# One-hot expert selection of a Flamingo block on one Trainium2 core: compares in 16 bits with token pairs innermost, the weight fold moved around the first choices, and runs of 8 tokens

## The chip, the cores and the metric

The kernel runs on one core of one Trainium2 chip. The metric is the device time of one launch in microseconds (us); the kernel before takes 4431.82 us, the median of 3 runs (4430.32 to 4437.95). One more execution was taken with the hardware profiler; all rows and stage times come from it.

## What is computed

Two Flamingo layers over x of 8 sequences, 512 tokens and 256 features. Each adds a tanh-gated cross-attention and a tanh-gated feed-forward to x. The change lies in the second feed-forward, a product-key memory of 64 x 64 = 4096 experts, cut here to what matters:

```python
q = einsum('bnd,de->bne', x, w_q)                       # 2 halves x 8 heads x 128
q = (q - mean) * rsqrt(var + eps) * gamma + beta        # statistics over all tokens
sim = einsum('pbnhd,hkpd->pbnhk', q, keys)              # 2 x 8 heads x 64 keys per token
sx, ix = top_k(sim[0], 8); sy, iy = top_k(sim[1], 8)
scores, pk = top_k(sx[..., :, None] + sy[..., None, :], 8)   # 8 of the 64 pairs of each head
indices = 64 * ix + iy, taken at pk                     # 64 experts per token
h = softmax(scores) * gelu_new(x . down_embed[indices])
out = sum over the 64 experts of h * up_embed[indices]
```

## The kernel before

**Stages.** `attention_phase` does everything up to the last feed-forward and, while it runs, computes the inner products of x with all 4096 `down` rows for seven of the eight sequences (`inner`, `expert_products`, L123), storing them to DRAM in `h_d`. `fold_phase` then does the same for the last sequence (`activations`, 16 calls, GELU straight into the tiles `gs`), and folds w_q, the batch statistics and the keys into one matrix `mk` and one row `crow` (matmuls into `y`, `sq`, `pw`, `pc`). The last stage walks over 16 blocks of 256 tokens, two tiles p of 128 tokens each, four steps u per tile.

**One step of the last stage.** `one_hot` (L1250, L1252) compares the tokens' 64 chosen first and second key numbers (`chT`) with 0..63 (`iota`) on VectorE (DVE), giving `m1` and `m2` of 128 x 1024 in fp32, and GpSimd (POOL) multiplies `m2` by the softmax weight (L1253). 32 matmuls of 64 x 64 (L1263) turn them into the weight of every expert for 16 tokens, `cf` in PSUM. `weigh` (L1272, DVE) multiplies the activations `gs` by them in place. `finish` (L1281) multiplies the previous block's `gs` by `up_sb`, in six pieces over steps 0 to 5 of a block; after step 5 `store` adds x and writes `out` (`fin`, L1296, L1299), and reads the next block's x rows (`xt`, L1293). For tiles ahead, `similar` makes the similarities (L1162, L1163, copied to `sim` by ScalarE, ACT, L1164), `top` finds 8 of 64 in 16 rows (L1175, L1176), `choose` 8 of 64 pairs in 8 rows (L1192, L1193) and `places` the key numbers (L1206 to L1239). `fetch` (L1304) loads four pieces c0 to c3 of the block after next from `h_d` into `gs` when `finish` has freed them, and `apply` (L1310) runs GELU on them on ACT.

**Order.** Only TensorE (PE) keeps the order in which the code is written; for the other engines and SP's DMA queue a scheduler fixes an order when the program is built, and each runs its own in sequence. In the built order ACT copies a tile's second `sim` half after the GELUs of c0 and c1. The DMAs of the queues take eight semaphores in turn, so each waits for the one eight places before it. Tokens are split over the two column halves of the PE array in runs of 32 (`s=32`), which fixes that `xt` and `out` move in DMAs of 32 rows, 8 each per block. The whole of `up` (two copies, 8.4 MB) is loaded from POOL's queue ahead of the fold, L1133.

Of the kernel before, what the change touches and what calls it, by code (L numbers as in the profile page):

```python
# [36 lines left out]
def kernel(  # L37
# [79 lines left out]
    def expert_products(ps, dw, xT):  # L117


        for k in range(NK):  # L120
            runs = xT[:, k, :].rearrange("p (r q s) -> p r q s", q=2, s=32)
            for q in range(2):
                nc.tensor.matmul(  # L123
                    ps[64 * q : 64 * q + 64, :], dw[:, k, :], runs[:, :, q, :],
                    start=(k == 0), stop=(k == NK - 1),
                )
# [905 lines left out]
    def fold_phase(ctx: ExitStack):  # L1032

        wp = ctx.enter_context(tc.tile_pool(name="wp", bufs=2))
        st = ctx.enter_context(tc.tile_pool(name="st", bufs=1))
        ps_h = ctx.enter_context(tc.tile_pool(name="ps_hl", bufs=2, space=PSUM))
        ps_y = ctx.enter_context(tc.tile_pool(name="ps_yf", bufs=2, space=PSUM))
        ps_s = ctx.enter_context(tc.tile_pool(name="ps_st", bufs=1, space=PSUM))

        xl = st.tile([P, NK, S], F32, name="xl")  # L1040
        nc.sync.dma_start(xl, xT_d[:, :, last * S : (last + 1) * S])
        bn_sb = st.tile([P, 32], F32, name="bn_sb")
        nc.scalar.dma_start(bn_sb, bn)
        kT = st.tile([P, 16, 64], F32, name="kT")
        nc.scalar.dma_start(kT, keysT)

        def activations(i4):

            dw = wp.tile([P, NK, 4, 64], F32, name="dwl")
            nc.sync.dma_start(dw, down[:, :, 4 * i4 : 4 * i4 + 4, :])  # L1050
            for i2 in range(2):
                ps = ps_h.tile([P, 2, 2 * P], F32, name="ps_hl")
                for ii in range(2):
                    expert_products(ps[:, ii, :], dw[:, :, 2 * i2 + ii, :], xl)
                for n in range(2):
                    i0 = 4 * i4 + 2 * i2
                    nc.scalar.activation(
                        gs[n][:, i0 : i0 + 2, :], ps[:, :, n * P : (n + 1) * P],
                        AF.Gelu_apprx_tanh,
                    )  # L1060


        sq = ps_s.tile([P, 16, 2], F32, name="sq")
        for n4 in range(4):
            wq = wp.tile([P, NK, 512], F32, name="wq")
            nc.scalar.dma_start(
                wq, pwq[:, 512 * n4 : 512 * (n4 + 1)].rearrange("(k p) n -> p k n", p=P)
            )
            z = wp.tile([P, NK, 512], F32, name="z")
# [1 line left out]
            for k in range(NK):
                y = ps_y.tile([P, 512], F32, name="y", tag="y")
                for k2 in range(NK):
                    nc.tensor.matmul(
                        y, gram[:, k2, k * P : (k + 1) * P], wq[:, k2, :],
                        start=(k2 == 0), stop=(k2 == NK - 1),
                    )
                nc.vector.tensor_tensor(z[:, k, :], y, wq[:, k, :], ALU.mult)
# [1 line left out]
            for i in range(4):  # L1080
                n = 4 * n4 + i
                for j, (src, by) in enumerate(((z, None), (wq, gram))):
                    for k in range(NK):
                        nc.tensor.matmul(
                            sq[:, n, j : j + 1], src[:, k, i * P : (i + 1) * P],
                            ones[:, 0:1] if by is None else by[:, k, D : D + 1],
                            start=(k == 0), stop=(k == NK - 1),
                        )
        mv = st.tile([P, 16, 2], F32, name="mv")
        nc.vector.tensor_scalar(mv, sq, 1.0 / (NT * P), None, ALU.mult)  # L1090

        sc = st.tile([P, 16], F32, name="bn_sc")
        sh = st.tile([P, 16], F32, name="bn_sh")
        nc.vector.tensor_tensor(sc, mv[:, :, 1], mv[:, :, 1], ALU.mult)
        nc.vector.tensor_tensor(sc, mv[:, :, 0], sc, ALU.subtract)
        nc.vector.tensor_scalar(sc, sc, 0.0, EPS_LN, ALU.max, ALU.add)
        nc.gpsimd.tensor_tensor(sc, sc, mhalf.to_broadcast([P, 16]), ALU.pow)
        nc.vector.tensor_tensor(sc, sc, bn_sb[:, 0:16], ALU.mult)
        nc.vector.tensor_tensor(sh, sc, mv[:, :, 1], ALU.mult)
        nc.vector.tensor_tensor(sh, bn_sb[:, 16:32], sh, ALU.subtract)  # L1100
        ks = st.tile([P, 16, 64], F32, name="ks")
        nc.vector.tensor_tensor(ks, kT, sc.unsqueeze(2).to_broadcast([P, 16, 64]), ALU.mult)
        kh = st.tile([P, 16, 64], F32, name="kh")
        nc.vector.tensor_tensor(kh, kT, sh.unsqueeze(2).to_broadcast([P, 16, 64]), ALU.mult)
# [2 lines left out]
        for h in range(2):
            pw = [ps_y.tile([P, 8, 64], F32, name="pw", tag="y") for _ in range(NK)]
            for q4 in range(2):
                wT = wp.tile([P, 4, D], F32, name="wT")  # L1110
                nc.scalar.dma_start(wT, pwqT[:, 8 * h + 4 * q4 : 8 * h + 4 * q4 + 4, :])
                for k in range(NK):
                    for i in range(4):
                        nc.tensor.matmul(
                            pw[k][:, 4 * q4 + i, :], wT[:, i, k * P : (k + 1) * P],
                            ks[:, 8 * h + 4 * q4 + i, :], start=True, stop=True,
                        )
            for k in range(NK):
                nc.vector.tensor_copy(
                    mk[:, k, 512 * h : 512 * h + 512].rearrange("p (n i) -> p n i", i=64), pw[k]  # L1120
                )
        for h in range(2):
            pc = ps_y.tile([P, 512], F32, name="pc", tag="y")
            nc.tensor.matmul(
                pc[0:1], ones[:, 0:1], kh[:, 8 * h : 8 * h + 8, :].rearrange("p n i -> p (n i)"),
                start=True, stop=True,
            )
            nc.vector.tensor_copy(crow[:, 512 * h : 512 * h + 512], pc[0:1])
# [22 lines left out]
    def similar(p, h):  # L1151
# [89 lines left out]
    def one_hot(p, u):

        at = cts[p].rearrange("p x (q s) -> p x q s", q=2)[:, :, :, 8 * u : 8 * u + 8]

        def spread(x):
            return at[:, x].unsqueeze(3).to_broadcast([P, 2, 8, 64])

        grid = iota.unsqueeze(1).unsqueeze(1).to_broadcast([P, 2, 8, 64])
        m1 = oh.tile([P, 2, 8, 64], F32, name="m1")
        nc.vector.tensor_tensor(m1, spread(0), grid, ALU.is_equal)  # L1250
        m2 = oh.tile([P, 2, 8, 64], F32, name="m2")
        nc.vector.tensor_tensor(m2, spread(1), grid, ALU.is_equal)  # L1252
        nc.gpsimd.tensor_tensor(m2, m2, spread(2), ALU.mult)  # L1253
# [61 lines left out]
    for p in range(2):
        for h in range(2):
            similar(p, h)
        for n0 in (0, 8):
# [81 lines left out]
```

## Time and profile before

| | us |
|---|---|
| median of the runs shown | 4431.82 |
| profiled execution, its own time | 4438.74 |
| its span, first to last instruction | 4436.9 |
| end of the attention stage (last `ps_g` matmul ended) | 3311.4 |
| first `sim` matmul of the last stage | 3458.6 |
| first `cf` matmul | 3510.6 |
| first `fin` | 3613.9 |
| last `cf` matmul / last `acc` matmul | 4400.8 / 4430.2 |
| busy: PE, DVE, ACT, POOL | 85%, 56%, 36%, 14% |

The page averages over stages with different limits: DVE is busy 56% of the whole, but 98.6% of the time from 3750 to 3900 us. Busy times by stretch, and instructions in order of time, are read below.

### The profile page before, as it was taken

The numbers are of one execution on the slowest core, as the hardware profiler recorded it, in microseconds if no ns is written. First come the engines' busy times: TensorE is split into PE (matmuls) and PEld (weight loads), VectorE is DVE, ScalarE is ACT, GpSimd is POOL, SyncE is SP. The second block draws the span as 40 slices with busy tenths as digits, with TensorE's granted clock in tenths as the row PEclk, the third lists the DMA queues.
The fourth block names the chain that finished last, engine by engine and source line by source line (L and its number), as shares of the span: only waits on it lengthen the run. The fifth ranks groups of instructions, "written<-read, shape, count | busy, mean of one in ns | idle before, by whom it ended". The sixth has DMA issues, their size and how long they took to land.

```text
span 4436.9 us, 74250 instructions
## 1 busy us (share of the span) xinstructions
PE 3779.7 (85%) x30697; PEld 1922.5 (43%) x30697; DVE 2473.8 (56%) x5662; ACT 1580.1 (36%) x2029; POOL 616.8 (14%) x613
## 2 busy tenths in 40 slices
PE   5678788889888998998898898789987589999998
PEld 2223332434334344434334434234445266666667
DVE  3455544454554454455445534553200699999995
ACT  2124343334443443453354343443431123333221
POOL 3210101020011012002001200000000122222222
PEclk7678998899999999999999999998997799999999
DMA  3201122123113313311321321103353022222221
GB/s 97 50 20 39 32 65 53 39 69 103 54 54 105 89 46 99 101 48 54 107 77 51 103 87 46 26 23 81 100 158 95 15 78 84 90 92 92 84 90 42
DMA packets 192254, 314.79 MB, mean 71 GB/s; under 512 B 20190, under 2 KB 145662, under 8 KB 184510
## 3 DMA queue, kind: packets, MB, share of 16 engines
q1 hardware_dynamic: 173468, 239.98, 18.0%
q0 software_dynamic: 15776, 65.02, 5.3%
q10 hardware_dynamic: 2672, 5.04, 0.4%
q8 instruction: 242, 3.96, 0.4%
q14 instruction: 96, 0.79, 0.1%
HBM read 220.93 MB, written 88.24 MB: 70 GB/s over the span
## 4 chain that ended last, share of the span: by engine, by line
PE 37%; DVE 17%; DMA 3%; ACT 1%; issue 1%; POOL 1%; SPq 0%; DVEq 0%; POOLq 0%; ACTq 0%
PE sc L331 10%; PE acc L1281 7%; PE ps_hd L123 6%; DVE nm L348 4%; PE av L391 3%; DVE m L1250 2%; DVE gs L1272 2%; DVE m L1252 2%; PE ps_y L707 1%; PE ps_hl L123 1%; DVE i L1176 1%; PE ps_h L690 1%; PE ps_sim L1162 1%; PE ps_q L293 1%; PE cf L1263 1%
## 5 line engine op out<-in xcount | busy, mean ns | idle before, releaser
L348 DVE TENSOR_REDUCE nm<-sc 128x2 f32<-128x1024 f32 x768 | 939.1, 1224 | 1047.0 <-PE sc L331 1043.2
L331 PE MATMUL sc<-ka,qa 32*128 32x512 f32 x3072 | 960.7, 684 | 297.4 <-DVE nm L348 284.4
L376 ACT ACTIVATE pr<-sc 128x1024 f32<-128x1024 f32 x768 | 785.9, 1024 | 1156.9 <-PE sc L331 1155.1
L331 PE MATMUL sc<-qa,ka 32*128 32x512 f32 x3072 | 917.8, 671 | 21.0 <-ACT pr L376 15.9
L331 PEld LDWEIGHTS sc<-ka,qa 32*128 32x128 f32 x3072 | 261.2, 194 | 722.7 <-DVE nm L348 535.8
L1281 PE MATMUL acc<-up_sb,gs 64*128 64x256 f32 x4096 | 489.9, 394 | 37.6 <-DVE gs L1272 37.6
L123 PE MATMUL ps_hd<-xT,dw 128*64 128x256 f32 x3584 | 439.0, 390 | 17.0 <-DMA dw<-in_down 6.5
L1281 PEld LDWEIGHTS acc<-up_sb,gs 64*128 64x128 f32 x4096 | 405.0, 195 | 93.3 <-DVE gs L1272 39.8
L391 PE MATMUL av<-pr,v 128*32 128x512 f32 x3072 | 436.6, 642 | 7.1 <-ACT pr L376 7.1
L1253 POOL TENSOR_TENSOR m<-m,chT 128x1024 f32<-128x1024 f32 x128 | 256.8, 2006 | 724.1 <-DVE m L1252 513.7
L123 PEld LDWEIGHTS ps_hd<-xT,dw 128*64 128x64 f32 x3584 | 247.1, 139 | 248.8 <-issue 117.9
L331 PEld LDWEIGHTS sc<-qa,ka 32*128 32x128 f32 x3072 | 246.8, 190 | 69.9 <-ACT pr L376 34.6
L823 ACT COPY hb<-ps_hd 128x512 f32<-128x512 f32 x224 | 130.8, 586 | 314.9 <-PE ps_hd L123 289.4
L542 ACT ACTIVATE pd<-mb,aT 128x512 f32<-128x512 f32 (+3 forms) x256 | 129.6, 553 | 211.2 <-PE cav L549 108.7
L391 PEld LDWEIGHTS av<-pr,v 128*32 128x32 f32 x3072 | 62.0, 110 | 320.2 <-issue 298.7
L534 POOL TENSOR_SCALAR_AFFINE_SELECT mb<-mb 128x256 f32<-128x256 f32 x128 | 52.2, 408 | 1010.9 <-DMA mb<-nM_d 572.8
L1263 PE MATMUL cf<-m,m 64*64 64x64 f32 x8192 | 156.1, 228 | 34.5 <-DVE gs L1272 29.0
L1263 PEld LDWEIGHTS cf<-m,m 64*64 64x64 f32 x8192 | 138.9, 141 | 101.4 <-issue 84.8
L1250 DVE TENSOR_TENSOR m<-chT,iota 128x1024 f32<-128x1024 f32 x128 | 169.8, 1326 | 2.0 <-ACT chT L1239 2.0
L569 DVE SCALAR_TENSOR_TENSOR pd<-csc,pd 128x512 f32<-128x512 f32 (+3 forms) x256 | 115.9, 486 | 94.3 <-PE csc L564 77.5
L1196 ACT ACT_TABLE_LOAD x28 | 35.9, 1283 | 366.5 <-DVE w L1195 354.3
L564 PE MATMUL csc<-qT,cT 32*128 32x256 f32 (+3 forms) x512 | 150.8, 567 | 10.8 <-DVE pd L569 7.2
(218 smaller groups left out, 4330.9 us busy)
## 6 DMA issues: line engine op xcount, KB each, us to landing
h_d<-hb SPq DMA_DIRECT2D x224, 256.0 KB
gs<-h_d SPq DMA_DIRECT2D x56, 1024.0 KB
dw<-in_down SPq DMA_DIRECT2D x112, 256.0 KB
w1e<-in_w POOLq DMA_DIRECT2D x16, 1024.0 KB, 5.4
w2e<-in_w POOLq DMA_DIRECT2D x16, 1024.0 KB, 6.3
mb<-nM_d SPq DMA_DIRECT2D x32, 512.0 KB
qk_d<-pk SPq DMA_DIRECT2D x64, 256.0 KB
ws<-in_w SPq DMA_DIRECT2D x56, 256.0 KB
```

Source lines behind the costliest of these rows:

```text
L123: nc.tensor.matmul(ps[64 * q : 64 * q + 64, :], dw[:, k, :], runs[:, :, q, :], start=(k == 0), stop=(k == NK - 1),)
L331: nc.tensor.matmul(sc[:, i, :], lhs[r : r + 32, g, c * P : (c + 1) * P], rhs[r : r + 32, g, :], start=True, stop=True,)
L348: nc.vector.tensor_reduce(self.nm[:, c, 2 * half : 2 * half + 2, g], sc, AX.X, ALU.max, negate=True)
L376: nc.scalar.activation(self.pr[jj], sc, AF.Exp)
L391: nc.tensor.matmul(self.av[32 * j : 32 * j + 32, :], self.va[:, c, h * (self.hd + 1) : h * (self.hd + 1) + 32], pr[j // 2][:, j % 2, :], s ...
L542: nc.scalar.activation(pds[c][:, i, s0:], mb[:, i, s0:], AF.Exp, bias=aT[:, c, h : h + 1])
L564: nc.tensor.matmul(sc[i][:, s0:], cT[r : r + 32, g, s0 : s0 + P], qT[r : r + 32, g, s0:], start=True, stop=True,)
L823: nc.scalar.copy(hb.rearrange("p n i t -> p i n t"), ps.rearrange("p i (n t) -> p i n t", n=2),)
L1250: nc.vector.tensor_tensor(m1, spread(0), grid, ALU.is_equal)
L1253: nc.gpsimd.tensor_tensor(m2, m2, spread(2), ALU.mult)
L1263: nc.tensor.matmul(cf[64 * q : 64 * q + 64, h, s, :], m2[rows, q, s, :], m1[rows, q, s, :], start=True, stop=True,)
L1281: nc.tensor.matmul(accs[n][q], gs[n % 2][rows, i, :], up_sb[rows, i, :], start=(i == 0), stop=(i == 63),)
```

## The change

- **Fold.** `activations` for experts 0..5 stay in the fold; the other ten calls stand behind the similarities, `top` and `choose` of the first two tiles, five before each `places`. The fold's inputs are loaded at its start into the room of `up_sb`, and `up` is loaded afterwards in 16 DMAs of 0.5 MB on SP's queue, whose order is now that of the code in this phase. The column sums `pc` come right behind the statistics.
- **`crow`** becomes three bf16 rows that add up to the fp32 row, multiplied by bf16 ones.
- **`one_hot`** compares bf16 against bf16 into `o1`, `o2`, with a pair of tokens innermost; ACT copies `o1` to fp32 `m1`, POOL multiplies `o2` by the weight into fp32 `m2`. The buffers: `o1` 1, the others 2, where `m1` and `m2` had 3. The 64 x 64 matmuls read `m1` and `m2` with a step of two elements.
- **Small work** goes from DVE to ACT (`kf`, `iv`) and to POOL (`w`, the softmax product).
- **Runs of 8** (`s=8`) in place of 32: `xt` and `out` move in 32 DMAs each of 8 rows per block.

```diff
-            runs = xT[:, k, :].rearrange("p (r q s) -> p r q s", q=2, s=32)
+            runs = xT[:, k, :].rearrange("p (r q s) -> p r q s", q=2, s=8)
...
-        nc.tensor.matmul(ps, ones[0:1, :], crow[:, cols], start=False, stop=True)
+        nc.tensor.matmul(ps, ones3, crow[:, cols], start=False, stop=True)
...
-        nc.vector.tensor_tensor(w, sc, sc[:, :, 0:1].to_broadcast([P, 8, 8]), ALU.subtract)
+        nc.gpsimd.tensor_tensor(w, sc, sc[:, :, 0:1].to_broadcast([P, 8, 8]), ALU.subtract)
...
-        nc.vector.tensor_copy(kf, ku)
+        nc.scalar.copy(kf, ku)
-        nc.vector.tensor_copy(iv, i8)
+        nc.scalar.copy(iv, i8)
...
-            activations(2 * n4)
+            activations(n4)
...
-            activations(2 * n4 + 1)
...
-        for i4 in range(8, 12):
-            activations(i4)
...
-        for i4 in range(12, 16):
-            activations(i4)
-    for q in range(2):
-        nc.gpsimd.dma_start(up_sb[64 * q : 64 * q + 64], up)
...
+                pc[0:3], ones[:, 0:3], kh[:, 8 * h : 8 * h + 8, :].rearrange("p n i -> p (n i)"),
+                start=True, stop=True,
...
+        activations(4)
+        activations(5)
...
+        for p in range(2):
+            for h in range(2):
+                similar(p, h)
+            for n0 in (0, 8):
+                top(p, n0)
+            choose(p)
+        for p in range(2):
+            for i4 in range(5 * p + 6, 5 * p + 11):
+                activations(i4)
+            places(p)
+            for i in range(32 * p, 32 * p + 32, 8):
+                for q in range(2):
+                    nc.sync.dma_start(
+                        up_sb[64 * q : 64 * q + 64, i : i + 8, :], up[:, i : i + 8, :]
+                    )
+        for h in range(2):
+            similar(2, h)
...
-        nc.vector.tensor_tensor(m1, spread(0), grid, ALU.is_equal)
-        nc.vector.tensor_tensor(m2, spread(1), grid, ALU.is_equal)
-        nc.gpsimd.tensor_tensor(m2, m2, spread(2), ALU.mult)
+        def tokens(x):
+            x = x[:, 16 * u : 16 * u + 16].rearrange("p (v t) -> p v t", t=2)
+            return x.unsqueeze(2).to_broadcast([P, 8, 64, 2])
+        grid = iota.unsqueeze(1).to_broadcast([P, 8, 64, 2])
+        o1 = oh.tile([P, 8, 64, 2], BF16, name="o1", bufs=1)
+        nc.vector.tensor_tensor(o1, tokens(ci[:, 0]), grid, ALU.is_equal)
+        m1 = oh.tile([P, 8, 64, 2], F32, name="m1")
+        nc.scalar.copy(m1, o1)
+        o2 = oh.tile([P, 8, 64, 2], BF16, name="o2")
+        nc.vector.tensor_tensor(o2, tokens(ci[:, 1]), grid, ALU.is_equal)
+        m2 = oh.tile([P, 8, 64, 2], F32, name="m2")
+        nc.gpsimd.tensor_tensor(m2, o2, tokens(cw), ALU.mult)
...
-            for r in range(4):
-                row = t0 + 64 * r + 32 * q
+            for r in range(16):
+                row = t0 + 16 * r + 8 * q
```

More of the change, by code (lines that the diff above doesn't have):

```diff
@@ L1015 @@
     mk = p2.tile([P, NK, 1024], F32, name="mk")
-    crow = p2.tile([1, 1024], F32, name="crow")
+    crow = p2.tile([3, 1024], BF16, name="crow")
+    ones3 = p2.tile([3, P], BF16, name="ones3")
+    nc.vector.memset(ones3, 1.0)
     iota8 = p2.tile([P, 8], BF16, name="iota8")
-    iota = p2.tile([P, 64], F32, name="iota")
+    iota = p2.tile([P, 64, 2], BF16, name="iota")
     nc.gpsimd.iota(
@@ L1023 @@
     nc.gpsimd.iota(
-        iota, pattern=[[1, 64]], base=0, channel_multiplier=0,
+        iota, pattern=[[1, 64], [0, 2]], base=0, channel_multiplier=0,
         allow_small_or_imprecise_dtypes=True,
@@ L1030 @@
     tiles = [2 * n + i for n in blocks for i in range(2)]
[L1032 to L1069, printed above, removed]
-            activations(2 * n4)
[L1071 to L1078, printed above, removed]
-            activations(2 * n4 + 1)
[L1080 to L1104, printed above, removed]
-        for i4 in range(8, 12):
-            activations(i4)
[L1107 to L1128, printed above, removed]
-        for i4 in range(12, 16):
-            activations(i4)
@@ L1132 @@
-    for q in range(2):
-        nc.gpsimd.dma_start(up_sb[64 * q : 64 * q + 64], up)
-    ctx.enter_context(tc.manual_schedule(engines=ORDERED))
-    with ExitStack() as phase:
-        fold_phase(phase)
     tk = ctx.enter_context(tc.tile_pool(name="tk", bufs=2))
-    oh = ctx.enter_context(tc.tile_pool(name="oh", bufs=3))
-    ps_c = ctx.enter_context(tc.tile_pool(name="ps_c", bufs=2, space=PSUM))
-    ps_o = ctx.enter_context(tc.tile_pool(name="ps_o", bufs=1, space=PSUM))
+    oh = ctx.enter_context(tc.tile_pool(name="oh", bufs=2))
@@ L1228, in places @@
         nc.vector.reciprocal(sm, sm)
-        nc.vector.tensor_tensor(
+        nc.gpsimd.tensor_tensor(
             mlw[:, 2, 0, :].rearrange("p (h k) -> p h k", k=8), w,
@@ L1236, in places @@
             nc.tensor.transpose(tr[:, i, :], mlw[:, i].rearrange("p d k -> p (d k)"), ident)
-        ct = cts[p] = tk.tile([P, 3, 64], F32, name="chT", bufs=3)
-        nc.scalar.copy(ct[0:64], tr[0:64, 0:3, 0:64])
-        nc.scalar.copy(ct[64:128], tr[64:128, 0:3, 64:128])
-    def one_hot(p, u):
[L1243 to L1253, printed above, removed]
+        ci = tk.tile([P, 2, 64], BF16, name="ciT", bufs=3)
@@ new lines, in places, with fold_phase, room, activations @@
+        cw = tk.tile([P, 64], F32, name="cwT", bufs=3)
+        for h in range(2):
+            rows = slice(64 * h, 64 * h + 64)
+            nc.scalar.copy(ci[rows], tr[rows, 0:2, rows])
+            nc.scalar.copy(cw[rows], tr[rows, 2, rows])
+        cts[p] = (ci, cw)
+    def fold_phase(ctx: ExitStack):
+        wp = ctx.enter_context(tc.tile_pool(name="wp", bufs=2))
+        st = ctx.enter_context(tc.tile_pool(name="st", bufs=1))
+        ps_h = ctx.enter_context(tc.tile_pool(name="ps_hl", bufs=2, space=PSUM))
+        ps_y = ctx.enter_context(tc.tile_pool(name="ps_yf", bufs=2, space=PSUM))
+        ps_s = ctx.enter_context(tc.tile_pool(name="ps_st", bufs=1, space=PSUM))
+        def room(i, shape):
+            axes = dict(zip("ab", shape))
+            return up_sb[:, 4 * i : 4 * i + 4, :].rearrange(
+                "p x y -> p (x y)"
+            ).rearrange("p (a b) -> p a b", **axes)
+        xl = room(15, (NK, S))
+        nc.sync.dma_start(xl, xT_d[:, :, last * S : (last + 1) * S])
+        bn_sb = st.tile([P, 32], F32, name="bn_sb")
+        nc.scalar.dma_start(bn_sb, bn)
+        wqs = [room(n4, (NK, 512)) for n4 in range(4)]
+        for n4, wq in enumerate(wqs):
+            nc.scalar.dma_start(
+                wq, pwq[:, 512 * n4 : 512 * (n4 + 1)].rearrange("(k p) n -> p k n", p=P)
+            )
+        kT = room(14, (16, 64))
+        nc.scalar.dma_start(kT, keysT)
+        wTs = [room(6 + i, (4, D)) for i in range(4)]
+        for i, wT in enumerate(wTs):
+            nc.scalar.dma_start(wT, pwqT[:, 4 * i : 4 * i + 4, :])
+        def activations(i4):
+            dw = wp.tile([P, NK, 4, 64], F32, name="dwl")
+            nc.sync.dma_start(dw, down[:, :, 4 * i4 : 4 * i4 + 4, :])
+            for i2 in range(2):
+                ps = ps_h.tile([P, 2, 2 * P], F32, name="ps_hl")
+                for ii in range(2):
+                    expert_products(ps[:, ii, :], dw[:, :, 2 * i2 + ii, :], xl)
+                for n in range(2):
+                    i0 = 4 * i4 + 2 * i2
+                    nc.scalar.activation(
+                        gs[n][:, i0 : i0 + 2, :], ps[:, :, n * P : (n + 1) * P],
+                        AF.Gelu_apprx_tanh,
+                    )
+        sq = ps_s.tile([P, 16, 2], F32, name="sq")
+        for n4 in range(4):
+            wq = wqs[n4]
+            z = room(4 + n4 % 2, (NK, 512))
+            activations(n4)
+            for k in range(NK):
+                y = ps_y.tile([P, 512], F32, name="y", tag="y")
+                for k2 in range(NK):
+                    nc.tensor.matmul(
+                        y, gram[:, k2, k * P : (k + 1) * P], wq[:, k2, :],
+                        start=(k2 == 0), stop=(k2 == NK - 1),
+                    )
+                nc.vector.tensor_tensor(z[:, k, :], y, wq[:, k, :], ALU.mult)
+            for i in range(4):
+                n = 4 * n4 + i
+                for j, (src, by) in enumerate(((z, None), (wq, gram))):
+                    for k in range(NK):
+                        nc.tensor.matmul(
+                            sq[:, n, j : j + 1], src[:, k, i * P : (i + 1) * P],
+                            ones[:, 0:1] if by is None else by[:, k, D : D + 1],
+                            start=(k == 0), stop=(k == NK - 1),
+                        )
+        mv = st.tile([P, 16, 2], F32, name="mv")
+        nc.vector.tensor_scalar(mv, sq, 1.0 / (NT * P), None, ALU.mult)
+        sc = st.tile([P, 16], F32, name="bn_sc")
+        sh = st.tile([P, 16], F32, name="bn_sh")
+        nc.vector.tensor_tensor(sc, mv[:, :, 1], mv[:, :, 1], ALU.mult)
+        nc.vector.tensor_tensor(sc, mv[:, :, 0], sc, ALU.subtract)
+        nc.vector.tensor_scalar(sc, sc, 0.0, EPS_LN, ALU.max, ALU.add)
+        nc.gpsimd.tensor_tensor(sc, sc, mhalf.to_broadcast([P, 16]), ALU.pow)
+        nc.vector.tensor_tensor(sc, sc, bn_sb[:, 0:16], ALU.mult)
+        nc.vector.tensor_tensor(sh, sc, mv[:, :, 1], ALU.mult)
+        nc.vector.tensor_tensor(sh, bn_sb[:, 16:32], sh, ALU.subtract)
+        ks = room(10, (16, 64))
+        nc.vector.tensor_tensor(ks, kT, sc.unsqueeze(2).to_broadcast([P, 16, 64]), ALU.mult)
+        kh = room(11, (16, 64))
+        nc.vector.tensor_tensor(kh, kT, sh.unsqueeze(2).to_broadcast([P, 16, 64]), ALU.mult)
+        for h in range(2):
+            pc = ps_y.tile([P, 512], F32, name="pc", tag="y")
+            nc.tensor.matmul(
+                pc[0:3], ones[:, 0:3], kh[:, 8 * h : 8 * h + 8, :].rearrange("p n i -> p (n i)"),
+                start=True, stop=True,
+            )
+            t0, t1 = (st.tile([3, 512], BF16, name=f"t{i}") for i in range(2))
+            rest = st.tile([3, 512], F32, name="rest")
+            nc.vector.tensor_copy(t0, pc[0:3])
+            nc.vector.tensor_tensor(rest, pc[0:3], t0, ALU.subtract)
+            nc.vector.tensor_copy(t1, rest)
+            nc.vector.tensor_tensor(rest, rest, t1, ALU.subtract)
+            nc.vector.tensor_scalar(rest, rest, ident[0:3, 2:3], None, ALU.mult)
+            for i, t in enumerate((t0, t1)):
+                nc.vector.scalar_tensor_tensor(
+                    rest if i == 0 else crow[:, 512 * h : 512 * h + 512],
+                    t, ident[0:3, i : i + 1], rest, ALU.mult, ALU.add,
+                )
+        activations(4)
+        activations(5)
+        for h in range(2):
+            pw = [ps_y.tile([P, 8, 64], F32, name="pw", tag="y") for _ in range(NK)]
+            for q4 in range(2):
+                wT = wTs[2 * h + q4]
+                for k in range(NK):
+                    for i in range(4):
+                        nc.tensor.matmul(
+                            pw[k][:, 4 * q4 + i, :], wT[:, i, k * P : (k + 1) * P],
+                            ks[:, 8 * h + 4 * q4 + i, :], start=True, stop=True,
+                        )
+            for k in range(NK):
+                nc.vector.tensor_copy(
+                    mk[:, k, 512 * h : 512 * h + 512].rearrange("p (n i) -> p n i", i=64), pw[k]
+                )
+        for p in range(2):
+            for h in range(2):
+                similar(p, h)
[10 more added lines that the diff above has]
+                        up_sb[64 * q : 64 * q + 64, i : i + 8, :], up[:, i : i + 8, :]
+                    )
+        for h in range(2):
+            similar(2, h)
@@ new lines @@
+    ctx.enter_context(tc.manual_schedule(engines=ORDERED))
+    with ExitStack() as phase:
+        phase.enter_context(tc.manual_schedule(engines={mybir.EngineType.SP}))
+        fold_phase(phase)
+    ps_c = ctx.enter_context(tc.tile_pool(name="ps_c", bufs=2, space=PSUM))
+    ps_o = ctx.enter_context(tc.tile_pool(name="ps_o", bufs=1, space=PSUM))
+    def one_hot(p, u):
+        ci, cw = cts[p]
+        def tokens(x):
[10 more added lines that the diff above has]
+        nc.gpsimd.tensor_tensor(m2, o2, tokens(cw), ALU.mult)
@@ L1263, in weights_of @@
                     nc.tensor.matmul(
-                        cf[64 * q : 64 * q + 64, h, s, :], m2[rows, q, s, :], m1[rows, q, s, :],
+                        cf[64 * q : 64 * q + 64, h, s, :], m2[rows, 4 * q + s // 2, :, s % 2], m1[rows, 4 * q + s // 2, :, s % 2],
                         start=True, stop=True,
@@ L1290, in store @@
             fin = tk.tile([P, D], F32, name="fin")
-            for r in range(4):
-                row = t0 + 64 * r + 32 * q
+            for r in range(16):
+                row = t0 + 16 * r + 8 * q
                 nc.sync.dma_start(
-                    xt[32 * r : 32 * r + 32], x_d[NC * b + row // P, row % P : row % P + 32, :]
+                    xt[8 * r : 8 * r + 8], x_d[NC * b + row // P, row % P : row % P + 8, :]
                 )
             nc.vector.scalar_tensor_tensor(fin, accs[n][q], tg[:, 3:4], xt, ALU.mult, ALU.add)
-            for r in range(4):
-                row = t0 + 64 * r + 32 * q
-                nc.sync.dma_start(out[b, row : row + 32, :], fin[32 * r : 32 * r + 32])
+            for r in range(16):
+                row = t0 + 16 * r + 8 * q
+                nc.sync.dma_start(out[b, row : row + 8, :], fin[8 * r : 8 * r + 8])
     def fetch(n, c):
@@ L1314 @@
     NP = len(tiles)
[L1315 to L1318, printed above, removed]
-            top(p, n0)
-        choose(p)
-        places(p)
-    for h in range(2):
-        similar(2, h)
     one_hot(0, 0)
```

## Prediction

> **What bounds the kernel now.** I read the busy times by stretch first, since DVE's 56% is an average over stages. Columns: stretch and length, then busy time and instructions of PE, PEld, DVE, ACT and POOL, PE clock, DMA share, GB/s.
>
> ```profile
> 3310.00:3345.00 35.00, 19.04 (x111) 13.22 (x109) 1.97 (x4) 3.92 (x9) 1.45 (x4) 0.73 0.99 215
> 3345.00:3400.00 55.00, 40.78 (x243) 26.04 (x244) 2.77 (x4) 6.59 (x20) 0.00 (x0) 0.74 0.30 75
> 3458.00:3511.00 53.00, 28.48 (x70) 9.82 (x74) 36.91 (x204) 7.01 (x15) 6.39 (x3) 0.61 0.05 13
> 3511.00:3570.00 59.00, 31.39 (x624) 19.41 (x616) 58.79 (x219) 5.07 (x13) 15.21 (x8) 0.71 0.03 8
> 3750.00:3900.00 150.00, 137.12 (x2039) 100.13 (x2035) 147.95 (x526) 48.73 (x65) 39.94 (x20) 0.95 0.27 91
> ```
>
> The fold starts with the DMA engines full. From 3458 to 3511 PE waits for the first choices; in the last stage DVE is full and PE 91%. The rows of groups from 3630 to 4360 us say with what (busy us, mean ns):
>
> ```profile
> L1250 DVE TENSOR_TENSOR m<-chT,iota 128x1024 f32<-128x1024 f32 x101 | 135.1, 1337 | 0.0
> L1252 DVE TENSOR_TENSOR m<-chT,iota 128x1024 f32<-128x1024 f32 x102 | 123.6, 1212 | 0.0
> L1216 DVE TENSOR_TENSOR hot<-kf,iota 128x512 bf16<-128x512 bf16 x52 | 33.6, 688 | 0.9
> L1221 DVE TENSOR_TENSOR hot<-hot,iv 128x512 bf16<-128x512 bf16 x52 | 19.6, 419 | 0.0
> ```
>
> The waits give what held PE in the fold, and what SP's fetches wait for (total us, times, longest):
>
> ```profile
> PE ps_hl L123 <- DMA dwl<-in_down: 27.6, 2, 27.0
> SPq L1304 <- PE acc L1281: 397.0, 56, 15.3
> ```
>
> Last, the instructions in order of time, SP's from one `fin` to the next fetch and two from POOL and DVE:
>
> ```profile
> 3844.97 5.04 SPq L1299 DMA_DIRECT2D out_x<-fin  x8
> 3850.05 3.67 SPq L1293 DMA_DIRECT2D xt<-x_d  x8
> 3853.82 0.53 SPq L1156 DMA_DIRECT2D xTt<-xT_d  x1
> 3861.85 8.53 SPq L1304 DMA_DIRECT2D gs<-h_d  x2
> ...
> 3815.99 1.90 POOL L1253 TENSOR_TENSOR m<-m,chT 128x1024 f32<-128x1024 f32 x1 [8.85 <-DVE m L1252]
> 3816.87 2.10 DVE L1250 TENSOR_TENSOR m<-chT,iota 128x1024 f32<-128x1024 f32 x1
> ```
>
> SP idles 7.5 us before the fetch, so its queue has slack today. The `out` bursts at 3614.41 and 4358.72 are 13 blocks apart: **57.25 us a block** of two tiles.
>
> [...] L1221 takes 419 ns, L1216, whose `kf` has innermost step 0, 688. [...] Contiguous `acc` and runs of 32 at L123 are alike (376 and 379 ns median).
>
> **The change part by part.** I add to the profiled execution: span 4436.9 and 1.8 around it, 4438.7, which is 6.9 above the median.
>
> *Compares.* L1216 to L1221 is 269 ns for 512 elements, so 1024 save 0.53 us: 8 per tile, **4.3 us of DVE a tile**. Off DVE also go `iv` (0.12 from start to start, though 0.99 with its waits), `w` and the product (0.13 each) and `kf` (0.27): 0.65. DVE's rows, from start to start, sum to 26.9 a tile [...]. After: 22.0. New waits: `hot` now waits for ACT's `kf`, behind POOL's `w`, the exp (0.26) and a copy (0.3): 0.7. [...] `o2` stands ahead of `o1` in three of four steps of the built order, with POOL's 1.9 us beginning 0.15 after an `o2` ends; 0.5 to 2.4 a tile, I take 1.2. DVE: **23.9 a tile, 47.8 a block**.
>
> *PE.* Per tile: `acc` 128 x 0.114 = 14.6, `cf` 4 x 1.09, `sim` 2 x 2.9, `tr` 0.4 = 25.2. One bf16 pass for the `crow` matmul (two records and 1.1 us today) takes some 0.85 off each half: 23.5, 47 a block. Halved read rates in `cf` would add 4.4 a tile[...].
>
> *ACT, POOL.* Four copies of 1024 (1.04 like L1310) bring ACT from 9.3 to some 15 a tile. POOL's bf16 input with pairs innermost is unseen: 1.9 (taken) to 3.8 each[...]. Neither is full.
>
> *SP.* After `fin` the queue holds 32 `out`, 17 `xt`, fetch c0, 15 `xt`, `xTt`, fetch c1. Behind c1 wait, in ACT's order, its GELUs, a copy `m1`, four small copies and the second `sim` copy (1.05 x 2 + 1.0 + 1.2 + 0.6 = 4.9), and behind that DVE's `top`. With spacing s: c0 issues at 49s and lands 5.3 later (as c1 today: 3814.05 to 3819.3); the eighth `xt` after it takes its semaphore, so waits for the landing; then 8 `xt`, `xTt` 0.5, c1 at 57s + 5.8, landed at 57s + 11.1, `sim` copied 4.9 later. From there to the next `fin` DVE takes 17.65 today (3827.32 to 3844.97), less 4 x 0.53 and 0.65, plus 0.7: 15.6. The block is **57s + 31.7**. Spacing is 0.46 for 32 rows (3.67/8); 0.33 for 8-row DMAs in the attention stage (1.32/4, L303); 13 one-row loads took 4.77, 0.37 each, with a duration of 0.21[...]. I take 0.37: **52.8 a block**, above DVE and PE, so SP's loop is what is late next. Gain 4.45 x 13 blocks = **58**.
>
> *Fold.* Walked along PE from the end of attention, 3311.4. `xl` now needs `up_sb`'s room, free only then, and shares DMA with 4.7 MB on ACT's queue: first matmul 3319 (3314.6 today). Four rounds of 3.5 (`activations`) + 3.6 (`y`) + 1 (wait for `z`, which `activations` hides today) + 3.6 (`sq`), plus 4 of slow clock: 3370. Statistics to `kh` 6.7 (3409.8 to 3416.6, now with nothing beside) and `pc` 2: 3379. Two `activations` cold 9, beside them DVE's split (14 x 0.6), `pw` and `mk` 10: 3398. Four `sim` halves 2.3 each: 3408. Five `activations` 18: 3426; DVE's 21 us for the first two tiles run beside. The next `dwl` stands behind half of `up` on SP, 4.2 MB at 200 GB/s: wait 15. Five more 19: 3460. `xTt` of tile 2 stands behind the other half: wait 16. Two `sim` halves: first `cf` at **3482** instead of 3510.6, 28 earlier (0 to 60 as these waits double or vanish). To the first `fin`, 103 us today, two DVE-bound tiles and six steps save 13. Fold and start: **41**.
>
> *End.* 32 `out` where 8 take 3.57: 32 x 0.37 = 11.8, **+8**. Unhidden, as nothing follows.
>
> Sum: -41 - 58 + 8 = -91; 4438.7 becomes 4348, and on the scale of the median **4341**.
>
> **Rivals.** *Engines alone bind* (SP's spacing under 0.31, or the fetches early): DVE at 47.8 plus coupling of two nearly equal engines, 49.7 a block; -41 - 98 + 8 gives 4301. For it: SP waited 397 us for PE; against: 64 issues where there were 16. *A price eats the last stage's gain* (full-rate compares 1.21, slow POOL[...], slow `cf`): each is worth 2 to 4 us a tile and brings the block back to 57; -33 gives 4399. Against: L1221. *Slower, through SP*: the loop fin, 64 small DMAs, c1, ACT, `top`, fin is the bound at a spacing near today's. It undoes everything from 57s + 31.7 = 59.8, s = 0.49; at 0.55, near the 0.63 of the 5.04 us burst, the block takes 63 and the kernel 4432 + 75 - 33 = 4474. For it: that burst and 1.9 us maxima; against: fewer rows each. That the change does not do what it says would show as L1297 at 1.2 us: in the third case.
>
> **How the numbers follow.** SP's loop at 0.37: 0.45, 4341. Engines alone: 0.2, 4301. Gain eaten: 0.2, 4399. SP slower: 0.15, over 4440 mostly. A measurement tells 0.2% (9 us) from no change. The range 4285 to 4435 leaves out most of the slower case and little at the low end. Faster 0.82, same 0.05, slower 0.13.
>
> **What would show it.** Right: compares near 0.69 us, `crow` matmul one record; SP busy for over 20 us behind each `fin`, ACT's GELU waiting for DMA `gs`, DVE for `sim`, DVE under 95% busy in the last stage, blocks 52 to 54 us apart; first `cf` near 3482, with waits of `ps_hl` for `dwl` and `sim` for `xTt`; last `out` burst 12 us. Wrong: blocks of 57 or more, compares at 1.2, first `cf` after 3510, or an attention stage that ends after 3320 because runs of 8 slow L123.

## The result, and the profile after

The changed kernel takes 4370.61 us, median of 4 runs (4360.24 to 4379.6), against 4434.89 (4430.32 to 4440.0): ratio 0.9854, 95% interval 0.9829 to 0.9879, so **64 us or 1.5% faster**. A second set gave 0.9867 (0.9848 to 0.9885). The profiled execution took 4369.74, 69 less than that of before. Read off at the same places in both traces, the 69 are:

| stretch | before | after | difference | predicted |
|---|---|---|---|---|
| start to the end of attention | 3311.4 | 3295.9 | -15.5 | 0 |
| to the first `cf` | 199.1 | 181.8 | -17.3 | -28 |
| to the first `out` burst | 103.8 | 95.9 | -7.9 | -13 |
| 13 blocks | 13 x 57.25 | 13 x 54.54 | -35.3 | -58 |
| last two blocks | 72.4 | 72.5 | 0 | 0 |
| from the last burst's start to the end | 5.8 | 12.9 | +7.1 | +8 |

The first row is not the change's. In the twelve traces of this study attention ends between 3282.8 and 3312.7, with runs of 8 at 3295.9 to 3312.7 and with runs of 32 at 3282.8, 3306.9 and 3311.4. Of the 15.5, 5.7 are one wait for a `dw` load in the trace of before. The matmuls with `dw`, which the runs of 8 touch, take 379 ns at the median in all twelve. Part of the spread goes with the TensorE clock that was granted up to there: 0.93 of full speed on the mean in the trace that ends first, 0.92 in the others. I therefore compare what follows attention: 1125.5 before, 1072.1 after, 1065.9 in the second trace of the changed kernel, which is **-53 to -60**, and agrees with the 64 and 56 of the medians of the two sets. The prediction's sum, -91, was some 30 us too good: 16 in the fold and start, 17 to 23 in the blocks.

Busy times by stretch of the changed kernel (the columns of the first fence of the prediction):

```profile
3296.00:3330.00 34.00, 22.23 (x114) 13.52 (x114) 3.07 (x6) 3.81 (x9) 0.91 (x2) 0.80 0.61 191
3330.00:3385.00 55.00, 46.54 (x292) 32.03 (x292) 16.55 (x30) 5.27 (x16) 2.89 (x1) 0.81 0.08 25
3385.00:3430.00 45.00, 30.86 (x200) 16.94 (x199) 33.12 (x175) 18.55 (x42) 5.70 (x6) 0.89 0.42 96
3430.00:3478.00 48.00, 27.33 (x195) 16.84 (x199) 1.82 (x17) 8.05 (x26) 0.00 (x0) 0.75 0.60 135
3600.00:4290.00 690.00, 624.21 (x10064) 469.75 (x10065) 624.96 (x2408) 338.14 (x508) 220.76 (x152) 0.94 0.29 94
```

From 3430 to 3478 nothing is full: PE 57%, DVE 4%, DMA 60%. In the last stage DVE, 99% busy before, is at 91%, PE at 90%, ACT at 49%: no engine is full by its own work. The groups of the last stage (busy us, mean ns, idle before and releasers):

```profile
L1303 POOL TENSOR_TENSOR m<-o,cwT 128x1024 f32<-128x1024 bf16 x102 | 207.1, 2041 | 186.2 <-PE cf L1313 162.0 <-DVE s L1069 14.9 <-DVE o L1301 9.3
L1301 DVE TENSOR_TENSOR o<-ciT,iota 128x1024 bf16<-128x1024 bf16 x102 | 119.3, 1170 | 16.1 <-POOL m L1303 16.1
L1299 ACT CAST m<-o 128x1024 f32<-128x1024 bf16 x102 | 106.0, 1039 | 92.3 <-DVE o L1297 85.7 <-PE cf L1313 3.4 <-DVE s L1069 3.0
L1297 DVE TENSOR_TENSOR o<-ciT,iota 128x1024 bf16<-128x1024 bf16 x103 | 89.4, 868 | 24.6 <-ACT m L1299 24.6
L1057 PE MATMUL ps_sim<-crow,ones 3*128 3x512 bf16 x50 | 20.6, 411 | 0.0
```

The compares take 0.68 us at the median, but 0.87 and 1.17 on the mean. Waits of the same stretch (total us, times, longest):

```profile
ACT gs L1360 <- DMA gs<-h_d: 61.8, 16, 8.4
POOL mlw L1123 <- DVE sm L1122: 49.5, 12, 4.1
PE ps_sim L1056 <- ACT sim L1058: 32.3, 12, 3.0
PE cf L1313 <- POOL m L1303: 28.4, 13, 5.2
```

GELU's wait for its fetch was 11.3 us in the same stretch of before; PE's waits for ACT's `sim` copy and for POOL's `m2` are new, 2.6 and 2.2 us a block. SP behind one `fin` (start, duration):

```profile
3847.38 11.11 SPq L1349 DMA_DIRECT2D out_x<-fin  x32
3858.53 6.74 SPq L1343 DMA_DIRECT2D xt<-x_d  x17
3865.43 0.35 SPq L1354 DMA_DIRECT2D gs<-h_d  x1
3865.83 8.54 SPq L1343 DMA_DIRECT2D xt<-x_d  x15
3874.41 0.53 SPq L1050 DMA_DIRECT2D xTt<-xT_d  x1
3875.05 0.54 SPq L1354 DMA_DIRECT2D gs<-h_d  x1
```

The eighth `xt` behind c0 waits 3.6 us for c0 to land (13 such waits in the trace, 31.4 us in all, the longest 4.0). c1 is issued 27.7 us behind the burst here, 24.9 to 29.4 in other blocks. Last, the three waits of PE for DMA in the fold:

```profile
3304.86 5.05 PE L123 MATMUL ps_hl<-up_sb,dwl 128*64 128x256 f32 x32 [9.01 <-DMA dwl<-in_down]
3435.47 13.19 PE L123 MATMUL ps_hl<-up_sb,dwl 128*64 128x256 f32 x96 [15.17 <-DMA dwl<-in_down]
3471.46 3.69 PE L1056 MATMUL ps_sim<-mk,xTt 128*128 128x512 f32 x4 [14.93 <-DMA xTt<-xT_d]
```

The second and third are where the prediction put them, 15 and 16 us.

### The profile page after: what moved, and what is told of

Read it like the earlier page. It is cut to its first block, busy times and chain, and to the rows that moved or that the text cites. A ratio compares the mean times of both kernels' runs of the same rounds, so it can differ in the third digit from the quotient of the medians.

```text
span 4368.0 us, 75138 instructions
## 1 busy us (share of the span) xinstructions
PE 3708.9 (85%) x30633; PEld 1893.8 (43%) x30633; DVE 2368.3 (54%) x5547; ACT 1729.0 (40%) x2289; POOL 636.0 (15%) x675
## 4 chain that ended last, share of the span: by engine, by line
PE 38%; DVE 12%; DMA 4%; ACT 2%; issue 2%; POOL 1%; SPq 1%; DVEq 0%; POOLq 0%; ACTq 0%
PE sc L331 10%; PE acc L1331 6%; PE ps_hd L123 6%; DVE nm L348 4%; PE av L391 3%; PE ps_sim L1056 2%; PE cf L1313 1%; PE ps_y L707 1%; PE ps_h L690 1%; DMA gs<-h_d 1%; PE ps_q L293 1%; PE ps_hl L123 1%; PE ps_p L282 1%; DVE gs L1322 1%; DVE i L1070 1%
## 5 line engine op out<-in xcount | busy, mean ns | idle before, releaser
L1331 PE MATMUL acc<-up_sb,gs 64*128 64x256 f32 x4096 | 468.8, 382 | 4.4 <-DVE gs L1322 4.4
L1331 PEld LDWEIGHTS acc<-up_sb,gs 64*128 64x128 f32 x4096 | 390.4, 188 | 52.7 <-DVE gs L1322 5.0
L1303 POOL TENSOR_TENSOR m<-o,cwT 128x1024 f32<-128x1024 bf16 x128 | 258.3, 2028 | 303.9 <-PE cf L1313 208.4
L1056 PE MATMUL ps_sim<-mk,xTt 128*128 128x512 f32 x256 | 148.4, 709 | 50.2 <-ACT sim L1058 35.3
L1299 ACT CAST m<-o 128x1024 f32<-128x1024 bf16 x128 | 133.1, 1040 | 142.4 <-DVE o L1297 102.9
L1322 DVE TENSOR_TENSOR gs<-cf,gs 128x1024 f32<-128x1024 f32 x128 | 153.5, 1200 | 17.0 <-PE cf L1313 16.1
```

Source lines behind the costliest of these rows:

```text
L1056: nc.tensor.matmul(ps, xt[:, k, :], mk[:, k, cols], start=(k == 0), stop=False)
L1299: nc.scalar.copy(m1, o1)
L1303: nc.gpsimd.tensor_tensor(m2, o2, tokens(cw), ALU.mult)
L1322: nc.vector.tensor_tensor(gv, cf.rearrange("p h s i -> p i h s"), gv, ALU.mult)
L1331: nc.tensor.matmul(accs[n][q], gs[n % 2][rows, i, :], up_sb[rows, i, :], start=(i == 0), stop=(i == 63),)
```

## The experiments

Each variant's block is the mean of 13, from the first to the fourteenth `out` burst of its trace; "after attention" is its time from the end of attention to the end. For the kernel before they are 57.25 and 1125.5, for the changed one 54.54 and 1072.1.

**The changed kernel again** (no edit).

> The changed kernel unaltered, for its scatter beside the variants. Blocks of 54 to 55 on the mean with a floor of 52.75, first cf 182 us and first fin 277 to 278 after the end of attention, 4360 to 4375. If its block mean is under 53.5, the gap of 1.6 to the kernel with one DMA each was one execution's accident and the queue behind fin costs nothing.

Measured: 4373.31 us, block 54.09, after attention 1065.9, first `cf` 181.9 behind attention. The block is above 53.5, so the gap to the next variant is not the accident of one execution.

**One DMA each for `xt` and `out`.**

```diff
...
-            for r in range(16):
-                row = t0 + 16 * r + 8 * q
-                nc.sync.dma_start(out[b, row : row + 8, :], fin[8 * r : 8 * r + 8])
+            ob = out[b, t0 : t0 + 2 * P, :].rearrange("(r q s) d -> q r s d", q=2, s=8)
+            nc.sync.dma_start(ob[q], fin)
```

> The changed kernel, with each of xt and out moved in one DMA of 128 rows (4 a block in place of 64). Theory SP: the queue behind fin holds the block at 54.5 us; without the 60 DMAs DVE's own work binds (49.4 us busy a block in the trace of the changed kernel, plus one or two of waits), blocks of 50 to 51, and the last burst shrinks from 10.8 to about 1 us: 13 x 4 + 9 = 60 us less than the changed kernel, about 4310. Theory engines: the block is held by DVE's compares, slowed by POOL's product, and by ACT's copies; blocks stay at 54 to 55, only the end gains 9: about 4361.

Measured: 4355.46 us, ratio 0.9811 (0.9795 to 0.9827); block 52.94, last burst to the end 4.1 in place of 12.9. Between the two theories: SP's queue costs 1.2 to 1.6 us a block (52.94 against 54.09 and 54.54), and without it the engines alone stop at 53, not at 50. Besides the DMAs one thing differs in the built order of DVE, ACT and POOL: a GELU now stands ahead of an `m1` copy on ACT, where it stood behind it; what that is worth was not measured. Its waits in the last stage:

```profile
PE ps_sim L1056 <- ACT sim L1058: 35.5, 12, 3.0
DVE o L1301 <- POOL m L1303: 14.9, 12, 1.2
ACT gs L1356 <- DMA gs<-h_d: 10.5, 7, 1.6
```

GELU's wait is back at the size of before; PE's wait for `sim` stays. What stands behind it, in order of time:

```profile
3955.88 0.29 POOL L1123 TENSOR_TENSOR mlw<-w,sm 128x64 f32<-128x64 f32 x1 [4.13 <-ACT gs L1356]
3956.13 3.76 POOL L1303 TENSOR_TENSOR m<-o,cwT 128x1024 f32<-128x1024 bf16 x2
...
3958.07 2.38 DVE L1301 TENSOR_TENSOR o<-ciT,iota 128x1024 bf16<-128x1024 bf16 x1 [1.24 <-POOL m L1303]
...
3960.36 0.68 DVE L1297 TENSOR_TENSOR o<-ciT,iota 128x1024 bf16<-128x1024 bf16 x1
...
3961.13 1.04 ACT L1299 CAST m<-o 128x1024 f32<-128x1024 bf16 x1 [4.19 <-DVE o L1297]
3962.09 0.58 ACT L1058 COPY sim<-ps_sim 128x512 f32<-128x512 f32 x1
...
3962.72 3.66 PE L1056 MATMUL ps_sim<-mk,xTt 128*128 128x512 f32 x4 [2.96 <-ACT sim L1058]
```

POOL's small product waits 4.13 us. It multiplies by DVE's reciprocal `sm`, which here ends 0.14 us before it starts; an ACT instruction that ends at the same time is named in its place, while 13 of the 25 waits of this kind in the stage are put down to `sm`. Two `m2` products stand behind it and run one after the other when it is done. `o2` waits 1.24 for a buffer of the first, then takes 2.38 beside the second, for 0.68 without one; `o1`, ACT's `m1` and ACT's `sim` copy follow late; PE waits 2.96 for the copy, and its next four `sim` matmuls take 3.66 where four take 1.98 without a wait before them. That is 4.6 us of PE in this block. The slow matmuls go with the granted clock, which the trace puts at half from 3962.70 to 3966.11 (busy times as before; the third number from the end is the clock):

```profile
3962.70:3966.11 3.41, 3.39 (x4) 1.18 (x4) 3.41 (x22) 3.38 (x7) 0.10 (x1) 0.50 0.54 154
```

Such a step to half stands beside 9 of the 13 waits of 2.96 us, and there the four take 2.98 to 3.78; in the other four blocks they take 1.98. These four blocks still take 52.5, so the late copy holds the block without the clock as well.

**Runs of 32 with the rest of the change.** `ci`, `cw` are written in the order of the runs by twice as many ACT copies.

```diff
-            runs = xT[:, k, :].rearrange("p (r q s) -> p r q s", q=2, s=8)
+            runs = xT[:, k, :].rearrange("p (r q s) -> p r q s", q=2, s=32)
...
-            nc.scalar.copy(ci[rows], tr[rows, 0:2, rows])
+            for q in range(2):
+                nc.scalar.copy(cv[:, :, :, q, :], tv[:, :, q])
...
```

> The changed kernel with runs of 32 in place of 8 (8 xt and 8 out DMAs a block; the choices are put in the order of the runs by twice as many small ACT copies, 0.9 us of ACT a tile). Theory SP: as with one DMA each, blocks of 50.5 to 52 and an end 7 us shorter, about 4315; the queue keeps its slack before the last fetches. Theory engines: blocks stay at 54 to 55, about 4363. Either way the matmuls with dw keep 379 ns and the attention stage ends between 3295 and 3312, as in the two traces there are.

Measured: 4347.61 us, ratio 0.9798 (0.9785 to 0.9810); block 52.86, after attention 1045.5. Again between the two theories, and the same floor from the other side: runs of 8 cost the changed kernel 20 to 27 us after attention (1065.9 and 1072.1 less 1045.5), 16 to 22 of them in the blocks and 7 at the end. The matmuls with `dw` keep 379 ns, as expected.

**Runs of 8 alone, on the kernel before.**

```diff
-        at = cts[p].rearrange("p x (q s) -> p x q s", q=2)[:, :, :, 8 * u : 8 * u + 8]
+        at = cts[p].rearrange("p x (u q s) -> p x u q s", u=4, q=2)[:, :, u]
...
```

> The kernel before with runs of 8 alone. Prediction's loop at the spacing of 0.35 us: c1 issued 26 us after fin, landed 6 later, sim copied 4 later, fin 17.65 later: 54, under DVE's 57.25, so blocks stay at 57 to 57.5 and only the end pays 7 us: about +7, 4442. Rival: the queue is already the bound at 32 rows less 7.5 us of slack, blocks go to 60 or more: +45 or more, 4480.

Measured: 4442.48 us, ratio 1.0021 (1.0009 to 1.0034); block 57.27, the end 7.1 longer. DVE's 57.25 hide the queue, as expected; once DVE is quicker the same DMAs cost two to three times as much.

**The new fold alone** (with the `crow` of the change; compares, small work and runs as before).

> The kernel before with the new fold and the bf16 crow, compares, small work and runs of 32 as before. First cf 182 us after the end of attention, as in the changed kernel (199 before), with the same two waits of 15 us for DMA; blocks of 57 (DVE), so 17 to 20 us less than before, about 4413. If the new fold owed its gain to the cheaper compares of its first tiles, under 10.

Measured: 4409.36 us, ratio 0.9943 (0.9926 to 0.9961), 25 less than before; first `cf` at 180.8, block 56.98, after attention 1101.8. The fold's part to the first `cf` is its own, 18. From here to runs of 32 are the compares and the small work: 56.98 to 52.86 a block, 54 us in 13.

**`w` and the softmax product back on DVE**, on the variant with one DMA each and on the changed kernel.

```diff
-        nc.gpsimd.tensor_tensor(w, sc, sc[:, :, 0:1].to_broadcast([P, 8, 8]), ALU.subtract)
+        nc.vector.tensor_tensor(w, sc, sc[:, :, 0:1].to_broadcast([P, 8, 8]), ALU.subtract)
...
-        nc.gpsimd.tensor_tensor(
+        nc.vector.tensor_tensor(
             mlw[:, 2, 0, :].rearrange("p (h k) -> p h k", k=8), w,
```

> The changed kernel with one DMA each for xt and out, and with w (L1089) and the softmax product (L1123) back on DVE. In the trace of one_dma the product waits in POOL's queue for DVE's reciprocal 4.1 us in every tile; two m2 products stand behind it and run together, o2 waits for a buffer and then takes 2.4 us beside the second, o1, ACT's m1 and ACT's sim copy follow late, and PE waits 3 us for the copy and restarts slowly, 1.9, once a block of 52.9. Theory queue: with the product on DVE (0.13 each for 2 ops a tile) this is gone: blocks of 49.5 to 50.5, no PE wait for ACT sim above 1 us, 13 x 2.9 = 38 less than one_dma, about 4318. [...] DVE is held by o1 and o2 at 0.88 and 1.18 us wherever POOL's product falls; blocks stay at 52 to 53, within 10 of one_dma, 4350.

Measured: 4326.27 us, ratio 0.9751 (0.9728 to 0.9774); block 51.67, after attention 1026.2. The groups of its last stage:

```profile
L1301 DVE TENSOR_TENSOR o<-ciT,iota 128x1024 bf16<-128x1024 bf16 x97 | 68.6, 708 | 0.0
L1297 DVE TENSOR_TENSOR o<-ciT,iota 128x1024 bf16<-128x1024 bf16 x97 | 68.3, 704 | 17.0 <-ACT m L1299 17.0
```

The compares are at 0.70 and 0.71, not at the second theory's 0.88 and 1.18; PE's wait for `sim` is at 1.0 a block. The first theory's cause holds; of its gain of 2.9 a block not quite half came: PE works 48.0 of 51.67; the rest are waits of 1.0 to 1.5 us, each once a block, for the `sim` copy and twice for `weigh`'s `gs`. Eleven of the blocks take 51.4. The other two take 53.1: their waits are the same, but behind one of 1.46 us 44 `acc` matmuls take 6.71 in place of 5.02, with the granted clock at half for 3.4 us.

> The changed kernel with only w and the softmax product back on DVE; 32 xt and 32 out DMAs a block as in the change. If the prediction's loop through SP (57s + 31.7, 52 to 53 at the spacing of 0.35 to 0.37) is a bound of its own, blocks stay at 52 to 53.5, 15 to 25 us less than the changed kernel, about 4350, with ACT's GELU waiting for DMA gs and DVE or PE behind it. If the queue's delay only adds its share to what POOL's queue costs, blocks fall to 51 or less, 45 less, about 4325.

Measured: 4356.95 us, ratio 0.9808 (0.9783 to 0.9833); block 52.90, after attention 1052.6. Six of its 13 blocks take 51.4, as 11 of 13 do in the variant with one DMA each; the others take up to 56.2. SP's loop is thus no fixed bound at 52.8: its spacing varies, and it shows in the blocks where it is long. In the six, c1 is issued 25.0 to 26.2 us behind the start of the burst, in the four of 55.3 to 56.2 it is 26.4 to 27.7. The two costs add up: 54.3 (mean of two traces) with both, 52.9 with either, 51.7 with neither.

**Only the product back on DVE** (the second half of that edit), with one DMA each.

> one_dma with the softmax product alone back on DVE; w stays on POOL. Theory: the product, which waits for the reciprocal at the end of DVE's seven hot instructions, is what holds the two m2 products back; w waits less long behind (its scores are ready about 4 us earlier). Then the blocks are as in one_dma_small_dve, 51.4 to 51.9, and o2 takes under 0.8 us on the mean. Rival: w holds POOL as well, from the scores' last row on, and the bunching stays: 52.5 to 53, o2 near 1.1.

Measured: 4371.09 us, ratio 0.9869 (0.9850 to 0.9888); block 54.47. A miss for the first theory, and a longer block than its rival's:

```profile
3862.09 0.29 POOL L1089 TENSOR_TENSOR w<-psc 128x64 f32<-128x64 f32 x1 [9.17 <-DVE psc L1086]
3862.34 3.77 POOL L1303 TENSOR_TENSOR m<-o,cwT 128x1024 f32<-128x1024 bf16 x2
3862.44 1.85 DVE L1100 TENSOR_SCALAR ku<-ppk 128x64 uint32<-128x64 uint32 x1
3864.21 1.94 DVE L1101 TENSOR_SCALAR ku<-ppk 128x64 uint32<-128x64 uint32 x1
```

`w` now holds the pair of products back, and they run beside other victims: `ku` takes 1.85 on the mean for 0.19, its twin 0.56, L1115 0.89 for 0.42. Summed over all rows that are longer than in the quietest variant, POOL costs DVE 4.6 us a tile here, 2.8 with `w` and product on POOL, 1.1 with `w` and product on DVE; DVE's busy time a block is 53.3, 49.6 and 46.8. In this one PE hardly waits for `sim` (2.1 us in all), and DVE at 98% is the bound. So what the pair costs DVE and what it costs PE are two things, and the place of the pair decides which is paid.

**`up` spread over the fold**, on the variant with `w` and product on DVE and one DMA each.

```diff
+        pieces = {7: (0, 4), 8: (4, 6), 9: (6, 7), 10: (7, 9), 11: (9, 10), 12: (10, 12), 13: (12, 13), 14: (13, 14)}
...
+                for c in range(*pieces.get(i4, (0, 0))):
+                    up_piece(c)
...
-            for i in range(32 * p, 32 * p + 32, 8):
-                for q in range(2):
-                    nc.sync.dma_start(
...
```

> one_dma_small_dve with the 16 loads of up spread among the loads of dwl behind it (four after the seventh activations, then one or two after each), the last two after the third similarities, in place of two groups of eight. Theory: the waits of 15 us of ps_hl for dwl and of 15 of sim for xTt are the price of eight loads of 0.5 MB standing ahead on the same queue; they vanish, first cf 152 to 158 us after the end of attention in place of 182, 25 to 30 less than one_dma_small_dve. Rival: the same 8.4 MB have to pass in the same time and the waits come back in small pieces before each dwl: under 12 less.

Measured: **4299.65 us**, ratio 0.9686 (0.9661 to 0.9710), the quickest of all; first `cf` 155.8 behind attention, after attention 999.1. The waits of PE for DMA in the fold after its first: 3.46 and 1.69 for `dwl`, none for `xTt`. The waits of 15 us came from the queue's order, not from the bytes: the same 8.4 MB are loaded.

**Two buffers for `o1`**, on that.

```diff
-        o1 = oh.tile([P, 8, 64, 2], BF16, name="o1", bufs=1)
+        o1 = oh.tile([P, 8, 64, 2], BF16, name="o1")
```

> up_spread with two buffers for o1 in place of one. Theory: DVE's waits of o1 for ACT's m1 copy (1.4 us a block in one_dma_small_dve) go, and the rest of PE's waits (3.6 a block) shrinks with them: blocks of 50.5 to 51.2, 5 to 12 us less than up_spread, about 4291. Rival: what is left is the circle PE sim, ACT copy, DVE top, weigh, PE, in which o1's buffer is slack: blocks of 51.4 to 51.7, within 4 us.

Measured: 4323.44 us, ratio 0.9753 (0.9735 to 0.9770): slower, block 53.44, against both theories. `o1`'s wait for ACT hardly falls (13.3 us, for 17.0 in the variant with one DMA each and `w` and product on DVE, whose last stage is the same but for the buffer), while DVE's wait for the `sim` copy grows from 38.1 to 58.3. On PE one wait changes: where it waited 1.06 for the `sim` copy and 1.46 ahead of an `acc`, it now waits once, 2.79:

```profile
3931.55 8.07 PE L1337 MATMUL acc<-up_sb,gs 64*128 64x256 f32 x44 [2.79 <-DVE gs L1328]
3930.94:3937.77 6.83, 6.22 (x30) 5.01 (x32) 6.83 (x35) 0.19 (x1) 0.00 (x0) 0.50 0.01 3
```

The granted clock is at half beside this wait in 13 of 13 blocks, for 3.4 or 6.8 us, and beside the 1.46 in 2 of 13 without the second buffer. The 44 matmuls take 6.4 to 8.1 in place of 5.02, and the blocks are longer by just that: 54.4 less 3.0, 53.1 less 1.7 and 52.8 less 1.4 are all 51.4, the block without a step. So the loss is the clock behind one long wait. That the wait brings the step is read from their standing together; why the circle gathers two waits into one stays open.

## Why the prediction was right or wrong

**Right in sign and in its range, some 30 us too good; its account of what holds a block was wrong in part.**

*Fold and start*, -41 predicted, -25 measured. The waits of 15 and 16 for `dwl` and `xTt` came as written (15.2, 14.9). Too short were the first matmul (9.0 behind attention for 7.6), the four rounds, 56.8 for 51, and statistics with `pc`, 10.4 for 8.7: in the rounds 32 matmuls with `dw` took 5.05 to 6.18 us where later ones take 3.67, and the four of `pc` 3.57. The mean granted clock of the rounds is 0.83, which is worth up to some 10 us of 56.8 (an estimate: 0.17 of them), where the walk had "4 of slow clock"; `pc` takes 3.57 in the trace of before too, and 2 was misread. The first five `activations` took 24.2 for 18, as PE waits 0.3 to 2.9 at a time for ACT's GELUs. These stand behind the exp of `w` of each of the two tiles, which brings two table loads of 1.28 us and a wait for POOL's `w` of 0.7 and 1.4; the walk had no ACT in it. `pw`, `mk` and the similarities gave 5.5 back. The first `cf` is 11 later than the walk, 181.8 for 170.6. From there to the first `fin` DVE's work fell by 14.7, but its waits grew from 3.0 to 9.8, 6.8 of them for the `sim` copy: 7.9 saved for 13.

*Compares.* 0.68 at the median for 1.21 before: the 0.53 read off L1216 and L1221. Without the 0.7 of waiting and the 1.2 taken for what DVE loses beside POOL's products, the sum was 22.0 a tile; the trace has 49.4 busy a block less 2 x 2.7 of such loss, 22.0. The term of DVE's sum that was mis-sized is **DVE's loss beside POOL's products, taken at 1.2 a tile and measured at 2.7**, above the 2.4 given as its end. It was worked out for single products of 1.9 us; that the small product in POOL's queue would gather two of them was not seen. With `w` and the product on DVE it is 1.1. In the trace of before it shows as 2.10 us for 1.2 in an `m1` compare, in the changed kernel's variants as 2.38 for 0.68 in `o2` and 1.85 for 0.19 in `ku`; its mechanism was not shown. `MAX8`, `FIND_INDEX8` and `weigh`, which reads PSUM, kept 0.21, 0.22 and 1.20 to 1.21 in all eight traces whose DVE rows were listed.

*PE.* 48 a block for 47 with `w` and the product on DVE, 49.3 in the changed kernel, where the granted clock is 0.94 on the mean for 0.99. The `crow` matmul is one record of 0.385 at the median, where two took 1.1; the 0.85 taken off each half for it was the author's estimate, as the trace of before has no bf16 matmul. `cf` takes 218 ns at the median, as before: reading `m1` and `m2` with a step of two cost it nothing here.

*SP.* Spacing 0.34 to 0.42 in the bursts, c1 26.4 behind `fin` on the mean for 26.9: the queue's part of the loop was sized well. But I took the loop for the one bound, above engines at 49.7, and this is the step that failed: without the queue the block still takes 52.9. That this is so near the loop's 52.8 is luck. Of the 3.2 above 49.7, 1.3 are POOL's queue (1.1 between blocks without a step of the clock, 52.5 and 51.4): moving `w` and the product made it wait for DVE, which held back PE's `sim` and lengthened DVE's instructions (2.7 a tile, 1.1 with both on DVE). I had named the wait of `hot` for `kf` (0.18 each, for 0.7) and put that of POOL at nothing; its queue should have been walked like SP's. The other 2.0, still there at 51.7, are more coupling than the 1.9 that I had put on DVE's 47.8: PE works 48 and waits three times for the `sim` copy and `weigh`. What would shorten these waits no run here shows. So 54.5 is engines at 52.9 and 1.6 of SP's queue, not a loop of 52.8.

*End.* 10.8 for 11.8. *Rivals.* Engines alone at 49.7 is reached by no variant; slower through SP did not come, its break-even of 0.49 is above the spacing of every burst; part of the third case, DVE's loss beside POOL's products, is what took the missing gain.

## What to carry to other kernels

When small work moves to another engine, walk that engine's queue: what it waits for there, what stands behind it, and what those run beside when they are let go together. A cost that one full engine hid (64 small DMAs at 8 us) can show once that engine is relieved (20 to 27). Look at the granted clock before calling a wait cheap: here one wait of 2.79 us cost more than two of 1.06 and 1.46. Long transfers issued in one group ahead of small ones that were due cost two waits of 15 us here; spread between them, 5 us in all.

## What was not expected of the hardware

- Beside POOL's 128 x 1024 product even short DVE instructions are long: `ku` of 128 x 64 took 1.85 us on the mean for 0.19, the softmax product 1.09 for 0.23.
- Pieces of 8 rows need no DMA of their own: from the start of the last burst to the end of the span, two DMAs of 16 x 8 rows took 4.1 us, eight of 32 rows 5.8, 32 of 8 rows 12.9.
- The granted clock stood at half for 3.4 or 6.8 us beside 9 of 13 waits of PE of 2.96 us and 13 of 13 of 2.79, but beside 2 of 13 of 1.46.
- The end of attention, with the same matmuls but for the runs of 8 or 32, wandered by 30 us in 12 traces, and by 17 in the nine with runs of 8.
